# Copies out of PSUM kept back on ScalarE until the next step of another generator: a four-layer sparse graph kernel

## Chip, cores, metric

One core of one Trainium2 chip. The metric is device time in microseconds of one execution; lower is better.

## The reference, cut to what matters

```python
def _L0_gnn_ref(adj_matrix, h, Wq, Wk, Wv, Wo, bo, ...):       # also layers 2 and 3
    scores = einsum('bnhd,bmhd->bhnm', Q, K) / sqrt(HEAD_DIM)   # 8 heads of 16
    attn = softmax(where(adj == 0, -inf, scores))
    x = layer_norm(h + (attn @ V) @ Wo + bo)
    return layer_norm(x + relu(x @ W1 + b1) @ W2 + b2)
def _L1_gnn_ref(x, adj, W, a_src, a_dst, ...):                  # graph attention, then layer norm
```

x is (16, 1024, 128) in float32; a row of adj has about 8 neighbours in 1024. The kernel sorts the nodes by degree and gathers only the neighbours.

## The kernel before

Work goes in 64 units: 4 layers, 2 groups of graphs, 8 tiles of 128 nodes (t = 0 has the highest degrees, 7 the lowest; those with t from 3 to 6 are called quick). In a unit, VectorE forms products, sums and weighted products of gathered rows. The *tails* of the unit before run between them: output projection, norm, feed-forward, norm, projection for the next layer. A tail is a Python generator, one for each half (A and B) of the graphs, and B is one step behind A. The order in which they emit instructions is the order in which the traces show them on an engine (ScalarE has A's copy ahead of B's scalings, at 1688.05 and 1688.73 us).

```python
def normed(y):
    ...                                           # squares with sums, on ScalarE
    yield
    nc.gpsimd.tensor_tensor(rstd, total, power, ALU.pow)
    yield
    for i in range(GH):                           # "the four scalings", L422
        nc.scalar.activation(z[:, i, :], y[:, i, :], AF.Copy, scale=rstd[:, i : i + 1])
    return z

def turned(z, dst, gain=None, shift=None):
    ps = bank([P, GH, P])
    for i in range(GH):
        nc.tensor.transpose(ps[:, i, :], z[:, i, :], ident)
    if gain is None:
        nc.scalar.copy(dst, ps)                   # L431
    else:                                         # L433
        nc.scalar.activation(dst, ps, AF.Identity, bias=shift, scale=gain)
# ... (cut)
def attention_tail(l, g, t, h, o):
    for _ in range(h):                            # half B one step later
        yield
    # ... output projection, normed (cut)
    turned(z, x1, p["ln1_g"], p["ln1_b"])
    yield
    for f in range(F):                            # feed-forward: matmul L479, relu L483
        ...
    # ... second layer, normed (cut)
    yield from finish(...)                        # turned(z, xn, ...), then project(): kv, L371/L375
# ... (cut)
def exponentials(i):
    nc.vector.tensor_reduce(sc, ...)              # L614
    nc.scalar.activation(ex, sc, AF.Exp, ...)     # L618; weighted() on VectorE (L639) needs ex
# ... (cut)
def advance(gens):
    for gen in list(gens):
        if next(gen, "end") == "end":
            gens.remove(gen)
```

Of the kernel before, what the change touches and what calls it, by code (L numbers as in the profile page):

```python
# [15 lines left out]
AF = mybir.ActivationFunctionType  # L16
# [5 lines left out]
D = 128  # L22
# [23 lines left out]
GH = G // HF  # L46
# [30 lines left out]
def sparse_path(ctx: ExitStack, tc: tile.TileContext, a: dict, out: bass.AP, flag):  # L77


    nc = tc.nc  # L80
# [6 lines left out]
    def bank(shape):  # L87
        return banks.tile(shape, F32, tag="ps", name="ps")
# [270 lines left out]
    srcs = {}  # L359


    def project(l, g, t, h, x):

        nc.sync.dma_start(kept[l, g][t, :, h, :], x.rearrange("p g n -> p (g n)"))
        table = tables[l, g][t * P : (t + 1) * P, :]
        if LAYERS[l][1] is ATTN:
            kv = twos.tile([P, 2, GH, D], F32, tag="kv", name="kv")
            for i in range(0, GH, 2):
                ps = bank([P, 2, 2 * D])
                for k in range(2):  # L370
                    nc.tensor.matmul(  # L371
                        ps[:, k, :], x[:, i + k, :], w[LAYERS[l][0], "Wkv"],
                        start=True, stop=True,
                    )
                nc.scalar.copy(  # L375
                    kv[:, :, i : i + 2, :].rearrange("p c g d -> p g c d"),
                    ps.rearrange("p g (c d) -> p g c d", d=D),
                )
                yield
            nc.sync.dma_start(  # L380
                table.rearrange("p (c x) -> p c x", c=2)[:, :, h * GH * D : (h + 1) * GH * D],
                kv.rearrange("p c g d -> p c (g d)"),
            )
            return
        kv = twos.tile([P, GH * D + GH], F32, tag="kv", name="kv")
        if h == 0:
            srcs[g, t] = const.tile([P, G], F32, name=f"src{g}{t}")
        for i in range(0, GH, 2):
            ps = bank([P, 2, D + 2])
            for k in range(2):  # L390
                nc.tensor.matmul(ps[:, k, :], x[:, i + k, :], wg, start=True, stop=True)
            nc.scalar.copy(
                kv[:, i * D : (i + 2) * D].rearrange("p (g d) -> p g d", d=D), ps[:, :, :D]
            )
            to = GH * D + i
            nc.scalar.copy(
                kv[:, to : to + 2].rearrange("p (g o) -> p g o", o=1), ps[:, :, D : D + 1]
            )
            at = h * GH + i
            nc.scalar.copy(  # L400
                srcs[g, t][:, at : at + 2].rearrange("p (g o) -> p g o", o=1), ps[:, :, D + 1 :]
            )
            yield

        nc.sync.dma_start(table[:, h * GH * D : (h + 1) * GH * D], kv[:, : GH * D])
        nc.sync.dma_start(table[:, ROW + h * GH : ROW + (h + 1) * GH], kv[:, GH * D :])
# [18 lines left out]
    def turned(z, dst, gain=None, shift=None):  # L425

        ps = bank([P, GH, P])
        for i in range(GH):
            nc.tensor.transpose(ps[:, i, :], z[:, i, :], ident)  # L429
        if gain is None:  # L430
            nc.scalar.copy(dst, ps)  # L431
        else:
            nc.scalar.activation(dst, ps, AF.Identity, bias=shift, scale=gain)  # L433

    def over_graphs(v):
        return v.rearrange("p (o d) -> p o d", o=1).to_broadcast([P, GH, D])
# [17 lines left out]
    def attention_tail(l, g, t, h, o):  # L454
        layer = LAYERS[l][0]
        p = {n: w[layer, n] for n in ATTN if (layer, n) in w}
        xt = xs[l, g, t][:, h]
        for _ in range(h):
            yield
        oT = twos.tile([P, GH, P], F32, tag="oT", name="oT")  # L460
        turned(o, oT)
        yield
        ps = ybanks.tile([P, GH, D], F32, tag="yps", name="yps")
        for i in range(GH):
            nc.tensor.matmul(ps[:, i, :], oT[:, i, :], p["Wo"], start=True, stop=False)  # L465
            nc.tensor.matmul(ps[:, i, :], xt[:, i, :], centre, start=False, stop=True)
        yield
        y = twos.tile([P, GH, D], F32, tag="y", name="y")
        nc.vector.tensor_tensor(y, ps, over_graphs(p["bo"]), ALU.add)
        yield  # L470
        z = yield from normed(y)
        yield
        x1 = twos.tile([P, GH, P], F32, tag="oT", name="x1")
        turned(z, x1, p["ln1_g"], p["ln1_b"])
        yield
        f1 = ones_.tile([P, F, GH * P], F32, tag="f1", name="f1")
        for f in range(F):
            ps = bank([P, GH * P])
            nc.tensor.matmul(  # L479
                ps, p["W1"][:, f * P : (f + 1) * P], x1.rearrange("p g n -> p (g n)"),  # L480
                start=True, stop=True,
            )
            nc.scalar.activation(f1[:, f, :], ps, AF.Relu, bias=p["b1"][:, f : f + 1])  # L483
        yield
        ps = ybanks.tile([P, GH, D], F32, tag="yps", name="yps")
        for i in range(GH):
            for f in range(F):
                nc.tensor.matmul(  # L488
                    ps[:, i, :], f1[:, f, i * P : (i + 1) * P], p["W2"][:, f, :],
                    start=(f == 0), stop=False,  # L490
                )
            nc.tensor.matmul(ps[:, i, :], x1[:, i, :], centre, start=False, stop=True)  # L492
        yield
        z = yield from normed(ps)
        yield
        yield from finish(l, g, t, h, z, p["ln2_g"], p["ln2_b"])
# [40 lines left out]
    def is_attention(u):  # L537
        return LAYERS[units[u][0]][1] is ATTN
# [12 lines left out]
    def queries(u):  # L551

        l, g, t = units[u]
        if not is_attention(u):
            ps = bank([P, J, G])
            for j in range(J):
                nc.tensor.matmul(ps[:, j, :], rep_of(j, True), srcs[g, t], start=True, stop=True)
            ofs[u] = smalls.tile([P, J, G], F32, tag="of", name="of")
            nc.scalar.copy(ofs[u], ps)
            return  # L560
        qs[u] = reps.tile([P, J, ROW], F32, tag="qr", name="qr")
        for h in range(HF):
            q = ones_.tile([P, GH * D], F32, tag="q", name="q")
            ps = bank([P, GH, D])
            for i in range(GH):
                nc.tensor.matmul(
                    ps[:, i, :], xs[l, g, t][:, h, i, :], w[LAYERS[l][0], "Wq"],
                    start=True, stop=True,
                )
            nc.scalar.copy(q, ps.rearrange("p g d -> p (g d)"))  # L570
            yield
            pss = []
            for j in range(J):
                ps = bank([P, GH * D])
                nc.tensor.matmul(ps, rep_of(j), q[32 * j : 32 * j + 32], start=True, stop=True)  # L575
                pss.append(ps)
            for j in range(J):
                nc.scalar.copy(qs[u][:, j, h * GH * D : (h + 1) * GH * D], pss[j])  # L578
            yield

    def gathered(i):
# [22 lines left out]
    def exponentials(i):  # L604
# [8 lines left out]
        if is_attention(u):  # L613
            nc.vector.tensor_reduce(  # L614
                sc[:, :n, :], prs[i][0][:, :n, :].rearrange("p k (a d) -> p k a d", d=HD),
                mybir.AxisListType.X, ALU.add,
            )
            nc.scalar.activation(ex, sc[:, :n, :], AF.Exp, scale=1.0 / HD**0.5)  # L618
        else:
            nc.vector.tensor_tensor(  # L620
                sc[:, :n, :], es[i][:, :n, ROW:], ofs[u][:, j : j + n, :], ALU.add
            )
            nc.vector.scalar_tensor_tensor(
                sc[:, :n, :], sc[:, :n, :], SLOPE, sc[:, :n, :], ALU.mult, ALU.max
            )
            nc.scalar.activation(ex, sc[:, :n, :], AF.Exp)
# [45 lines left out]
    def divided(u):  # L672

        l, g, t = units[u]
        heads, d = (H, HD) if is_attention(u) else (1, D)
        den = bank([P, G * heads])
        for r, n in enumerate(ROUNDS[t]):
            for j in range(n):
# [25 lines left out]
    slow = []  # L704

    def advance(gens):
        for gen in list(gens):
            if next(gen, "end") == "end":
                gens.remove(gen)

    pace = [0.0, 0.0]

    def others():
        pace[0] += pace[1]
        while pace[0] >= 1.0:
            advance(tails)
            pace[0] -= 1.0
        if fronts:
            advance(fronts)
        elif slow:  # L720
            advance(slow)

    with tc.manual_schedule():
        for _ in first(0):
            pass
        loaded(0)
        loaded(1)
        for _ in queries(0):
            pass
        slow.append(first(1))  # L730
        for i in range(AHEAD):
            gathered(i)
# [2 lines left out]
        for i in range(len(parts) + 1):  # L735
# [43 lines left out]
            if ends:  # L779

                while fronts:
                    advance(fronts)
        while tails:
            advance(tails)
        for _ in closing:
# [437 lines left out]
```

## Time and profile before

| | us |
|---|---|
| time, median of 4 | 3033.95 (3027.94 to 3037.83) |
| VectorE busy, TensorE busy | 2150, 2125 |
| ScalarE busy, GpSimd busy | 1424, 1478 |
| VectorE's idle before L639, waiting for `ex` of L618 | 333 |

A wait line reads: engine and line that waited, who ended the wait, us in total, number of waits, the longest. A timeline line reads: start, length, engine, line, operation, out<-in, shape, and in square brackets the idle just before and its releaser. The lines themselves stand in the prediction.

### The profile page before, as it was taken

The page shows a single profiled execution, that of the slowest core. Times are in us where ns is not written, and L with a number is a line of the kernel's source. Part 1 is how long each engine was busy: PE and PEld are TensorE (multiplying, and loading weights), DVE is VectorE, ACT ScalarE, POOL GpSimd, SP SyncE. Part 2 cuts the span into 40 slices and gives each one's busy share as a digit, 9 for nine tenths or more (in the row PEclk, how much of TensorE's full clock was granted, in tenths as well). Part 3 has the DMA queues.
Part 4 walks back from the last instruction along what each step waited for, and adds up shares of the span by engine and source line. Part 5 has one row for each costly group of instructions (what it writes and reads, how often), then busy time and mean ns, then how long its engine had stood idle before and what let it go on. Part 6 is the DMA issues. An engine that isn't in the chain of part 4 may idle for free.

```text
span 3034.5 us, 35305 instructions
## 1 busy us (share of the span) xinstructions
PE 2124.9 (70%) x12569; PEld 1325.2 (44%) x12569; DVE 2150.0 (71%) x1493; ACT 1424.2 (47%) x4468; POOL 1478.1 (49%) x1086
## 2 busy tenths in 40 slices
PE   1365767776777786766577887777877676766766
PEld 1343444543554443434245554555544444334444
DVE  7505768768887666675798767887678877778772
ACT  1033445563556544435345664456543555334454
POOL 0123435443444568685335443354435577466673
PEclk9986888887888888988788988889887888787887
DMA  1057766545555468777665654656546553355540
GB/s 56 12 181 287 304 215 236 204 169 217 223 225 179 171 210 288 256 272 282 221 238 216 228 205 179 271 218 230 200 183 245 198 216 145 144 219 210 195 144 22
DMA packets 171144, 615.36 MB, mean 203 GB/s; under 512 B 44472, under 2 KB 47928, under 8 KB 122462
## 3 DMA queue, kind: packets, MB, share of 16 engines
q0 software_dynamic: 99584, 480.93, 43.4%
q1 hardware_dynamic: 71376, 132.10, 11.9%
q8 instruction: 101, 1.65, 0.2%
q14 instruction: 83, 0.68, 0.1%
HBM read 650.67 MB, written 100.73 MB: 248 GB/s over the span
## 4 chain that ended last, share of the span: by engine, by line
PE 40%; DVE 15%; ACT 14%; POOL 11%; issue 10%; DMA 8%; another core or an unknown queue 0%; SPq 0%; POOLq 0%; DVEq 0%; ACTq 0%
PE ps L479 7%; PE yps L488 6%; PE ps L429 5%; ACT z L413 5%; POOL e L591 5%; PE acc L666 5%; POOL rstd L419 4%; DVE sc L614 4%; DMA xg<-in_x,places 3%; DVE pr L639 3%; PE ps L371 3%; DVE pr L600 3%; ACT qr L578 3%; PE yps L465 3%; PE yps L492 3%
## 5 line engine op out<-in xcount | busy, mean ns | idle before, releaser
L591 POOL DMA_INDIRECT e<-table,idx x656 | 886.1, 1351 | 448.1 <-DVE pr L639 263.4
L639 DVE TENSOR_TENSOR pr<-e,ex 128x2048 f32<-128x2048 f32 (+1 forms) x344 | 760.1, 2216 | 338.7 <-ACT ex L618 333.4
L419 POOL TENSOR_TENSOR rstd<-total,power 128x4 f32<-128x4 f32 x224 | 359.9, 1608 | 753.4 <-ACT z L413 718.9
L600 DVE TENSOR_TENSOR pr<-e,qr 128x2048 f32<-128x2048 f32 (+1 forms) x258 | 565.1, 2190 | 195.1 <-ACT qr L578 138.1
L666 PE MATMUL acc<-pr,marks 128*32 128x512 f32 x2624 | 467.7, 701 | 146.5 <-DVE pr L639 136.6
L614 DVE TENSOR_REDUCE sc<-pr 128x128 f32<-128x2048 f32 (+1 forms) x258 | 561.9, 2178 | 0.0
L429 PE MATMUL ps<-ident,z 128*128 128x128 f32 x768 | 199.4, 368 | 246.5 <-ACT z L422 246.5
L429 PEld LDWEIGHTS ps<-ident,z 128*128 128x128 f32 x768 | 126.5, 172 | 396.2 <-ACT z L422 325.7
L371 PE MATMUL ps<-Wkv,xT 128*128 128x256 f32 x768 | 244.5, 466 | 41.5 <-ACT xT L431 21.2
L479 PE MATMUL ps<-x,W 128*128 128x512 f32 x384 | 241.1, 761 | 41.8 <-ACT x L433 41.8
L488 PE MATMUL yps<-W,f 128*128 128x128 f32 x1536 | 258.5, 287 | 13.0 <-ACT f L483 11.0
L666 PEld LDWEIGHTS acc<-pr,marks 128*32 128x32 f32 x2624 | 89.4, 120 | 398.5 <-issue 213.8
L488 PEld LDWEIGHTS yps<-W,f 128*128 128x128 f32 x1536 | 212.5, 197 | 69.9 <-ACT f L483 44.3
L483 ACT ACTIVATE f<-ps,b 128x512 f32<-128x512 f32 x192 | 131.4, 687 | 230.8 <-PE ps L479 230.0
L578 ACT COPY qr<-ps 128x512 f32<-128x512 f32 x384 | 197.6, 596 | 74.9 <-PE ps L575 74.7
L413 ACT ACTIVATE z<-y,root 128x128 f32<-128x128 f32 x512 | 198.5, 396 | 50.6 <-DVE y L506 35.4
L575 PE MATMUL ps<-q,rep 32*128 32x512 f32 x768 | 169.7, 679 | 67.4 <-ACT oT L431 41.3
L371 PEld LDWEIGHTS ps<-Wkv,xT 128*128 128x128 f32 x768 | 166.2, 231 | 91.2 <-ACT xT L431 29.3
L618 ACT ACTIVATE ex<-sc 128x128 f32<-128x128 f32 (+1 forms) x258 | 81.1, 314 | 253.6 <-DVE sc L614 236.1
L465 PE MATMUL yps<-Wo,oT 128*128 128x128 f32 x768 | 180.2, 322 | 7.5 <-ACT oT L431 6.9
L375 ACT COPY kv<-ps 128x512 f32<-128x512 f32 x192 | 112.5, 587 | 140.9 <-PE ps L371 129.4
L413 ACT ACTIVATE z<-yps,root 128x128 f32<-128x128 f32 x384 | 135.6, 368 | 77.2 <-PE yps L492 77.2
(128 smaller groups left out, 2977.8 us busy)
## 6 DMA issues: line engine op xcount, KB each, us to landing
table<-kv SPq DMA_DIRECT2D x96, 512.0 KB
kept<-xT SPq DMA_DIRECT2D x128, 256.0 KB
x<-kept SPq DMA_DIRECT2D x64, 512.0 KB
e<-table,idx POOLq DMA_INDIRECT x656
table<-kv SPq DMA_DIRECT2D x32, 256.0 KB
edges<-in_adj SPq DMA_DIRECT2D x8, 512.0 KB
W<-in_L_gnn_W SPq DMA_DIRECT2D x6, 128.0 KB
xg<-in_x,places POOLq DMA_INDIRECT x32
```

Source lines behind the costliest of these rows:

```text
L371: nc.tensor.matmul(ps[:, k, :], x[:, i + k, :], w[LAYERS[l][0], "Wkv"], start=True, stop=True,)
L413: nc.scalar.activation(z[:, i, :], y[:, i, :], AF.Square, scale=D**-0.5, bias=root, accum_out=total[:, i : i + 1],)
L419: nc.gpsimd.tensor_tensor(rstd, total, power, ALU.pow)
L429: nc.tensor.transpose(ps[:, i, :], z[:, i, :], ident)
L479: nc.tensor.matmul(ps, p["W1"][:, f * P : (f + 1) * P], x1.rearrange("p g n -> p (g n)"), start=True, stop=True,)
L488: nc.tensor.matmul(ps[:, i, :], f1[:, f, i * P : (i + 1) * P], p["W2"][:, f, :], start=(f == 0), stop=False,)
L578: nc.scalar.copy(qs[u][:, j, h * GH * D : (h + 1) * GH * D], pss[j])
L591: nc.gpsimd.indirect_dma_start(out=es[i][:, k, :], out_offset=None, in_=tables[l, g][:, :], in_offset=bass.IndirectOffsetOnAxis(ap=idx[:, ...
L600: nc.vector.tensor_tensor(prs[i][0][:, :n, :], es[i][:, :n, :ROW], qs[u][:, j : j + n, :], ALU.mult)
L614: nc.vector.tensor_reduce(sc[:, :n, :], prs[i][0][:, :n, :].rearrange("p k (a d) -> p k a d", d=HD), mybir.AxisListType.X, ALU.add,)
L639: nc.vector.tensor_tensor(prs[i][k0 // 2][:, :m, :].rearrange("p k (a d) -> p k a d", d=d), es[i][:, k0 : k0 + m, base : base + ROW].rearr ...
L666: nc.tensor.matmul(accums[u][32 * j : 32 * j + 32, h, :], marks[:, CHUNK[t, r, j], :], tiles[j // 2][:, j % 2, h * GH * D : (h + 1) * GH * D],
```

## The change

The intent: a copy out of PSUM (the `ps` that TensorE's matmuls write) has to wait for TensorE (50.0 us of ScalarE's idle before L433 in the kernel before), and ScalarE, which works in order in the trace (the `ex` at 1708.31 us began only after two copies, with its sums done since 1702.93), waits with it. So the copy is kept back and given to ScalarE later, at the next opening of a step (`advance`) or just ahead of the next attention exponential, so that other ScalarE work can go first.

```diff
+    pending = []
+    def flush():
+        while pending:
+            pending.pop(0)()
+    def later(fn, *args, **named):
+        pending.append(lambda: fn(*args, **named))
...
-            nc.scalar.activation(dst, ps, AF.Identity, bias=shift, scale=gain)
+            later(nc.scalar.activation, dst, ps, AF.Identity, bias=shift, scale=gain)
... (likewise the copies of kv, oT, f1, q, qr, of)
+            flush()
             nc.scalar.activation(ex, sc[:, :n, :], AF.Exp, scale=1.0 / HD**0.5)
...
     def advance(gens):
+        flush()
         for gen in list(gens):
... (flush also in others, divided, queries; others steps its front directly)
```

## The prediction

> **What bounds the kernel now.** I read the page first (parts 1, 2, 4, 5), then who waited for whom, then the timelines of ScalarE, TensorE, GpSimd and VectorE in one stretch that repeats.

> ```profile
> PE 2124.9 (70%) x12569; PEld 1325.2 (44%) x12569; DVE 2150.0 (71%) x1493; ACT 1424.2 (47%) x4468; POOL 1478.1 (49%) x1086
> PE 40%; DVE 15%; ACT 14%; POOL 11%; issue 10%; DMA 8%; another core or an unknown queue 0%; SPq 0%; POOLq 0%; DVEq 0%; ACTq 0%
> ```

> No engine is full, and the chain that ended last passes from engine to engine: the kernel is bound by waits between engines. The longest waits say which:

> ```profile
> DVE pr L639 <- ACT ex L618: 333.4, 128, 8.9
> PE ps L429 <- ACT z L422: 246.5, 94, 9.4
> ACT ex L618 <- DVE sc L614: 236.1, 59, 18.6
> ACT z L422 <- POOL rstd L419: 80.4, 49, 5.0
> PE ps L479 <- ACT x L433: 41.8, 46, 2.7
> ```

> VectorE waits 333.4 us for exponentials, in 128 of 258 places; the exponential itself waits for VectorE's sums only 59 times. So mostly an exponential is late because ScalarE works in order and has the layer tail's work in front of it. What delays a ScalarE instruction in front of such an exponential delays VectorE by as much. (The whole of L600's waits for `qr`, 138.1 us, has one of 103.1 us in it, the start.)

> [...] the `ex` at 1708.31 us began only after two copies, with its sums done since 1702.93. [...] The clock record agrees: it is only ever 1 or 0.5, and section 2 shows 0.7 to 0.9 as means. [...] the power (L419) took 1.04 us where it began ahead of a product of VectorE (1698.36 against 1698.44), 3.04 us where it began under one (L600, two inputs, 1702.85 to 1705.13). This makes some `rstd` late, which matters below.

> **The change part by part.** It adds and removes no work. I compared the order of the two programs on each engine, line numbers and buffer numbers left out. TensorE, VectorE, GpSimd and the DMA queue have the same instructions in the same order. On ScalarE, 132 of 4,123 instructions change places with something, in two ways.

> (a) 96 times (48 attention tails with `x1`, 32 with `xT` to the next layer, 16 graph tails) the copy of half A's transposes, with gain and shift (L433, 0.78 us), now stands after the four scalings of half B (L422, 1.27 us together) and no longer before them. Everywhere else a copy kept back meets only other copies kept back before the next opening, so the order stays.

> (b) 27 copies or so, nearly all in graph units, now stand after an exponential of graph attention instead of before it. VectorE waited for those exponentials only 5.0 us altogether (L639 on L626, 46 of them), so (b) is worth at most some 3 us.

> For (a), the first kind. ScalarE, then TensorE, then VectorE:

> ```profile
> 1686.35 1.28 ACT L422 ACTIVATE z<-y,rstd 128x128 f32<-128x128 f32 x4
> 1688.05 0.78 ACT L433 ACTIVATE x<-ps,ln_b,ln_g 128x512 f32<-128x512 f32 x1 [0.42 <-PE ps L429]
> 1688.73 1.27 ACT L422 ACTIVATE z<-y,rstd 128x128 f32<-128x128 f32 x4
> ...
> 1698.08 0.33 ACT L618 ACTIVATE ex<-sc 128x128 f32<-128x128 f32 x1
> ```

> ```profile
> 1688.88 1.99 PE L479 MATMUL ps<-x,W 128*128 128x512 f32 x4 [0.87 <-ACT x L433]
> 1690.70 0.60 PE L429 MATMUL ps<-ident,z 128*128 128x128 f32 x4
> ```

> ```profile
> 1698.44 2.29 DVE L639 TENSOR_TENSOR pr<-e,ex 128x2048 f32<-128x2048 f32 x1 [5.26 <-ACT ex L618]
> ```

> The idle that the change fills is the 0.42 us before the copy. But TensorE's next work, the feed-forward matmul at 1688.88, waits for this copy, and B's transposes stand behind that matmul in TensorE's own order: the row at 1690.70 has no wait for `z`. So finishing B's scaling earlier frees nobody, and the copy goes from 1688.05 to 1687.63 + 1.17 = 1688.80 us: 0.75 us later. From there everything is a chain (matmul, `f`, second layer, half B, squares, `ex`), and VectorE was already waiting 5.26 us at its end. So +0.75 us, whole.

> The second kind, where `rstd` of B is late (rows of ScalarE, GpSimd, TensorE):

> ```profile
> 1702.59 0.78 ACT L433 ACTIVATE xT<-ps,ln_b,ln_g 128x512 f32<-128x512 f32 x1 [0.42 <-PE ps L429]
> 1706.07 1.14 ACT L422 ACTIVATE z<-yps,rstd 128x128 f32<-128x128 f32 x4 [2.70 <-POOL rstd L419]
> 1707.09 0.60 ACT L375 COPY kv<-ps 128x512 f32<-128x512 f32 x1
> 1707.63 0.78 ACT L433 ACTIVATE xT<-ps,ln_b,ln_g 128x512 f32<-128x512 f32 x1
> 1708.31 0.30 ACT L618 ACTIVATE ex<-sc 128x128 f32<-128x128 f32 x1
> ```

> ```profile
> 1702.99 3.04 POOL L419 TENSOR_TENSOR rstd<-total,power 128x4 f32<-128x4 f32 x1
> ```

> ```profile
> 1703.42 1.13 PE L371 MATMUL ps<-Wkv,xT 128*128 128x256 f32 x4 [0.87 <-ACT xT L433]
> 1706.49 1.10 PE L429 MATMUL ps<-ident,z 128*128 128x128 f32 x4 [1.94 <-ACT z L422]
> ```

> Now the copy at 1702.59 was done in the shadow of the power. After the change it stands behind scalings that wait for the power: it starts at 1707.11, 4.5 us later. Then one after the other: copy to 1707.9, projection (L371, 1.13) to 1709.1, B's transposes (0.6 to 0.75) to 1709.7, B's copy (its next can start after 0.68), `ex` at 1710.4 instead of 1708.31. So +2.1 us, and VectorE was waiting there (3.51 us).

> I did this same shift for each of the 96 places from their own rows: new start of the copy, the projection's own length, 0.75 us for the transposes, less what time VectorE had left after that exponential before its L639.
> - 48 `x1`: 38 of them have VectorE waiting at the next exponential; 0.74 to 0.79 us in the quicker units, 0.91 to 1.17 in the others. Sum 33.1 us.
> - 32 `xT` of attention: 12 of the late kind at 1.6 to 3.0 us (24 us together), four with 1.7 us where VectorE waited only 0.16 us, the rest 0 to 1. Sum 37.7 us.
> - 16 graph tails: mostly 4 to 15 us of slack before the next use; sum 4.1 us.

> Together 75 us, an upper figure, as a later wait may give some back: I take nine tenths, 67 us. Less 3 us of (b). In the late kind TensorE now stands idle some 5 us between A's transposes and the projection, instead of 0.87 us, so its clock should halve there: projection and transposes twice as long, about 0.5 us in 12 places, 6 us. Sum: +70 us, 3035.6 + 70 = 3105.6; I say 3105.

> **The rivals.** *The intended gain*: ScalarE no longer stands before its queue's head waiting for TensorE. For it: the idle before L433 is 56 us, before L431 (L429's copies) 243 us. Against it: only the 0.42 us and the like before 96 copies of L433 is filled, 41 us in sum, and L431, L483 and L578 keep their place, as nothing given directly comes between them and the next opening. Even if all 41 us were gained, 2995; with losses half as large as I say, about 3035. *Slack swallows it*: VectorE is 71% busy, and gathers or the power may have been about to bound a unit anyway; the waits for gathered rows are only 56.1 us at L600 and 42.0 at L620, so I doubt it. Half of it swallowed: 3070. *PSUM*: copies given later hold the four banks longer. TensorE's order and the buffers' rotation are the same, and only copies of L433 are late; so nothing beyond the sum. *Runaway*: idle TensorE at half clock, in more places than 12, lengthens L479 and L488 in the chain; each 1% on TensorE's 40% of the chain is 12 us: 3130.

> **Range and chances.** All in all 3105, and 3065 to 3135 for 8 in 10: below, half of the loss hidden; above, the clock. The limit for slower by over 2% is 3096, close below my number: slower 0.61, within 2% 0.36, faster 0.03.

> **What would show it.** Right: all busy times but TensorE's within 1%; VectorE's wait at L639 for L618 up by about 60 us from 333; ScalarE's idle before L433 on TensorE down from 50.0 to near 10; L479's wait for `x` (41.8) up by 30 or more, and L371/L391's for `xT` (18.5 and 17.1) several times as long; in units like the one at 1702 us the copy of A directly behind B's scalings. Step by step wrong: if L639's wait stays at 333, the copies were not on the path; if L422's wait for `rstd` fell, the power isn't what makes B late; if the waits for gathered rows shrink by as much as L639's grow, slack swallowed it. A time under 3035 would mean that B's earlier scaling does free something that I hold to be behind the matmul.

## The result

3114.99 us, median of 4 (3110.0 to 3129.27), against 3033.95. The ratio is 1.0277, 95% interval 1.0236 to 1.0317: slower. A ratio here is the mean time of one kernel's fast runs over that of the other's in the same rounds, so not quite the ratio of the medians. The profiled run took 3108.2 us, 73.7 more than the profiled run of before.

In the changed kernel the copies all carry L369, the line of the helper, and other lines have moved: L433 and L483 are now L369, L422 is L435, L479 is L492, L371 is L380, L618 is L633, L639 is L654. The changed kernel's busy times first:

```profile
PE 2132.1 (69%) x12569; PEld 1332.7 (43%) x12569; DVE 2148.0 (69%) x1493; ACT 1420.3 (46%) x4468; POOL 1473.0 (47%) x1086
```

The busy times are the same to 0.4%, TensorE's 7 us longer. What grew is waiting; here is who waited for whom in the changed kernel:

```profile
DVE pr L654 <- ACT ex L633: 424.4, 125, 9.2
...
ACT ex L633 <- DVE sc L628: 238.6, 66, 18.8
...
PE ps L442 <- ACT z L435: 214.2, 80, 11.1
...
ACT z L435 <- POOL rstd L432: 123.8, 71, 8.2
...
PE ps L380 <- ACT xT L369: 85.6, 51, 5.4
...
PE ps L492 <- ACT x L369: 72.7, 47, 2.4
```

VectorE waits 91 us longer for exponentials (333.4 to 424.4), although the exponentials wait no longer for VectorE (236.1 to 238.6). The feed-forward matmul waits 31 us longer for `x` (41.8 to 72.7). The intended saving is there, and it is small: ScalarE's idle before L433 on the transposes fell from 50.0 to 15.6 us.

One quick unit of the changed kernel, the counterpart of those in the prediction (layer L2, tile 5). ScalarE's timeline around `x1`:

```profile
1801.88 2.45 ACT L435 ACTIVATE z<-y,rstd 128x128 f32<-128x128 f32 x8
1804.21 0.78 ACT L369 ACTIVATE x<-ps,ln_b,ln_g 128x512 f32<-128x512 f32 x1
1806.58 0.69 ACT L369 ACTIVATE f<-ps,b 128x512 f32<-128x512 f32 x1 [1.59 <-PE ps L492]
```

and around `xT`:

```profile
1818.47 1.16 ACT L435 ACTIVATE z<-yps,rstd 128x128 f32<-128x128 f32 x4
1823.53 1.14 ACT L435 ACTIVATE z<-yps,rstd 128x128 f32<-128x128 f32 x4 [3.90 <-POOL rstd L432]
1824.54 0.80 ACT L369 ACTIVATE xT<-ps,ln_b,ln_g 128x512 f32<-128x512 f32 x1
1827.51 0.59 ACT L369 COPY kv<-ps 128x512 f32<-128x512 f32 x1 [2.17 <-PE ps L380]
1828.36 0.78 ACT L369 ACTIVATE xT<-ps,ln_b,ln_g 128x512 f32<-128x512 f32 x1 [0.27 <-PE ps L442]
1829.04 0.30 ACT L633 ACTIVATE ex<-sc 128x128 f32<-128x128 f32 x1
```

Both halves are scaled in one run (x8), and only then is A's copy made. In the second stretch A's copy, which was made in the shadow of the power, stands behind scalings that wait 3.90 us for it. The same unit on TensorE and on VectorE:

```profile
1805.04 3.21 PE L492 MATMUL ps<-x,W 128*128 128x512 f32 x4 [1.50 <-ACT x L369]
...
1825.39 2.08 PE L380 MATMUL ps<-Wkv,xT 128*128 128x256 f32 x4 [5.23 <-ACT xT L369]
```

```profile
1815.90 2.29 DVE L654 TENSOR_TENSOR pr<-e,ex 128x2048 f32<-128x2048 f32 x1 [7.19 <-ACT ex L633]
...
1829.37 2.29 DVE L654 TENSOR_TENSOR pr<-e,ex 128x2048 f32<-128x2048 f32 x1 [6.78 <-ACT ex L633]
```

VectorE's two waits are 7.19 and 6.78 us where they were about 5.26 and 3.51. There is a second thing to see: the same four matmuls of L492 take 3.21 us instead of 1.98 or so, and those of L380 2.08 instead of 1.13. TensorE itself is slower here: over these two rows the granted clock is 0.60 and 0.50, over the rows of L479 and L371 in the prediction 1.00.

To see where the time went I took each unit's length from VectorE's timeline (from its division `o<-acc` to the next unit's, the stretch in which its tails run), added up by kind of unit and compared with the kernel before. "Predicted" is the sum of the places in that group as worked out for the prediction, ahead of its last corrections (the total: 75 us).

| units | before, us | predicted | changed | e1 | e3 (x1) | e4 (xT) |
|---|---|---|---|---|---|---|
| L0, t 0-2 (6) | 319.9 | +8.3 | +11.5 | +1.2 | +5.4 | +8.0 |
| L0, t 3-6 (8) | 327.6 | +17.2 | +19.2 | +0.2 | -0.7 | +16.6 |
| L2, t 0-2 (6) | 289.2 | +13.8 | +17.6 | +0.6 | +7.9 | +14.4 |
| L2, t 3-6 (8) | 327.3 | +20.4 | +31.5 | -0.5 | +21.7 | +21.5 |
| L3, t 0-2 (6) | 306.8 | +5.8 | +1.3 | -0.9 | -0.2 | -0.8 |
| L3, t 3-6 (8) | 326.6 | +5.4 | +10.2 | -0.1 | +11.5 | 0.0 |
| L1, graph (16) | 425.3 | +4.1 | -8.6 | -3.6 | +3.4 | +3.5 |

(e1, e3 and e4 are experiments below. The units with t = 7 and the lead-in are left out; they scatter by up to 10 us. Together with the end they are 9 us shorter in the changed kernel and 8 in e1, so the column "changed" sums to 83 us where the profiled runs differ by 74.)

### The profile page after: what moved, and what is told of

It is laid out like the page before. It is cut to its first block, busy times and chain, and to the rows that moved or that the text cites. A ratio compares the mean times of both kernels' runs of the same rounds, so it can differ in the third digit from the quotient of the medians.

```text
span 3108.2 us, 35279 instructions
## 1 busy us (share of the span) xinstructions
PE 2132.1 (69%) x12569; PEld 1332.7 (43%) x12569; DVE 2148.0 (69%) x1493; ACT 1420.3 (46%) x4468; POOL 1473.0 (47%) x1086
## 4 chain that ended last, share of the span: by engine, by line
PE 36%; ACT 17%; DVE 12%; POOL 11%; issue 9%; DMA 6%; POOLq 0%; DVEq 0%; SPq 0%; ACTq 0%
PE ps L492 7%; ACT z L426 6%; PE yps L501 6%; PE acc L681 5%; POOL rstd L432 5%; ACT z L435 5%; POOL e L605 5%; DVE sc L628 4%; DVE pr L654 3%; PE ps L380 3%; DVE pr L614 3%; DMA e<-table,idx 3%; PE ps L442 3%; ACT qr L369 3%; PE yps L505 3%
## 5 line engine op out<-in xcount | busy, mean ns | idle before, releaser
L654 DVE TENSOR_TENSOR pr<-e,ex 128x2048 f32<-128x2048 f32 (+1 forms) x344 | 760.7, 2218 | 429.3 <-ACT ex L633 424.4
L614 DVE TENSOR_TENSOR pr<-e,qr 128x2048 f32<-128x2048 f32 (+1 forms) x258 | 565.6, 2192 | 196.5 <-ACT qr L369 144.3
L681 PE MATMUL acc<-pr,marks 128*32 128x512 f32 x2624 | 460.9, 692 | 136.1 <-DVE pr L654 126.0
L380 PE MATMUL ps<-Wkv,xT 128*128 128x256 f32 x768 | 250.6, 475 | 86.2 <-ACT xT L369 85.6
L492 PE MATMUL ps<-x,W 128*128 128x512 f32 x384 | 249.8, 786 | 72.7 <-ACT x L369 72.7
L369 ACT ACTIVATE f<-ps,b 128x512 f32<-128x512 f32 x192 | 131.4, 687 | 285.1 <-PE ps L492 285.0
L501 PEld LDWEIGHTS yps<-W,f 128*128 128x128 f32 x1536 | 213.0, 197 | 68.5 <-ACT f L369 42.1
L369 ACT COPY kv<-ps 128x512 f32<-128x512 f32 (+2 forms) x320 | 140.2, 460 | 208.4 <-PE ps L380 162.2
L369 ACT COPY qr<-ps 128x512 f32<-128x512 f32 x384 | 197.5, 596 | 75.3 <-PE ps L589 72.6
L380 PEld LDWEIGHTS ps<-Wkv,xT 128*128 128x128 f32 x768 | 168.8, 235 | 137.3 <-ACT xT L369 106.3
L633 ACT ACTIVATE ex<-sc 128x128 f32<-128x128 f32 (+1 forms) x258 | 81.1, 314 | 249.4 <-DVE sc L628 238.6
L435 ACT ACTIVATE z<-y,rstd 128x128 f32<-128x128 f32 x512 | 160.4, 394 | 32.4 <-POOL rstd L432 32.3
```

The source lines that it names most:

```text
L369: pending.append(lambda: fn(*args, **named))
L380: nc.tensor.matmul(ps[:, k, :], x[:, i + k, :], w[LAYERS[l][0], "Wkv"], start=True, stop=True,)
L492: nc.tensor.matmul(ps, p["W1"][:, f * P : (f + 1) * P], x1.rearrange("p g n -> p (g n)"), start=True, stop=True,)
L501: nc.tensor.matmul(ps[:, i, :], f1[:, f, i * P : (i + 1) * P], p["W2"][:, f, :], start=(f == 0), stop=False,)
L614: nc.vector.tensor_tensor(prs[i][0][:, :n, :], es[i][:, :n, :ROW], qs[u][:, j : j + n, :], ALU.mult)
L654: nc.vector.tensor_tensor(prs[i][k0 // 2][:, :m, :].rearrange("p k (a d) -> p k a d", d=d), es[i][:, k0 : k0 + m, base : base + ROW].rearr ...
```

## The experiments

Theory: the loss is the 96 places in which B's scalings now stand ahead of A's copy. Rivals: the other effects of keeping copies back (part (b), PSUM banks, new waits); slack; and TensorE's clock. Every kernel was run beside the kernel before on one chip; the twelve fell into three groups, in which the kernel before had medians of 3028.9 (e1, e3, e4, e7), 3035.0 (e5, e6, e9, e10) and 3028.1 us (e8, e11, e12, e13).

### e1: copies ahead of the scalings again, all else as changed

```diff
+        flush()
         for i in range(GH):
             nc.scalar.activation(z[:, i, :], y[:, i, :], AF.Copy, scale=rstd[:, i : i + 1])
```

> The changed kernel with one line more: all copies kept back are given before half B's four scalings. This puts back the 96 places of part (a) exactly and keeps part (b), everything else as changed. My theory (the loss is the 96 places): within 10 us of the kernel before, 3025 to 3045, VectorE's wait for the attention exponential back to about 333 us (before) from 424 (changed). Rival (part (b), PSUM banks held longer, or semaphores of the new order cost something by themselves): it stays near 3115, or stops in between.

Measured: 3030.4 us, ratio 1.0004 (0.9978 to 1.003). The wait in the first fence of the result is back:

```profile
DVE pr L655 <- ACT ex L634: 330.0, 124, 8.9
```

One line undoes the whole loss. The rest of the change (27 or so copies behind graph exponentials, the openings, the longer hold on the banks) is worth nothing that can be measured (0.3% would have shown).

### e3 and e4: the two kinds of place alone

```diff
-            nc.scalar.activation(dst, ps, AF.Identity, bias=shift, scale=gain)
+            give(nc.scalar.activation, dst, ps, AF.Identity, bias=shift, scale=gain)
 # e3: give=later for x1 alone; e4: give=later for xn alone; every other copy given at once
```

> Of all copies only the 48 pairs of x1 are kept back, the rest is given at once as in the kernel before. Theory: 33 us of loss, all of the small kind (0.75 to 1.17 us each), ratio 1.011, about 3067. Rival (only the places with a late power cost anything, and small shifts are swallowed by slack): ratio 1.000. Rival (feed-forward is where it all happens): the whole 80 us, ratio 1.027.

Measured: 3080.1 us, ratio 1.0163 (1.0136 to 1.019): 49 us, not 33.

> Of all copies only those of xT (to the next layer, 32 pairs of attention and 16 of graph tails) are kept back. Theory: 42 us from the places and some 6 us from TensorE's half clock, ratio 1.015 (3080), and the wait of the scalings for the power up from 80 to about 124 us, as in the changed kernel. With e3 the two should sum to the changed kernel's 80 us if the places are independent. Rival (slack swallows xT): ratio 1.000 to 1.005.

Measured: 3085.18 us, ratio 1.0179 (1.0151 to 1.0206): 54 us, somewhat over the 48. The scalings' wait for the power is 120.5 us, near the 124 expected.

Neither rival holds: both kinds cost, and neither is swallowed as a whole. But e3 costs half as much again as its places, and the two do not add up (1.63 and 1.79% against 2.77%). The table shows where: e3's eight quick units of L2 lost 21.7 us, and the same eight units of L0, with the same instructions up to the next projection, lost nothing. The busy view by stretch shows what is different there. Columns are stretch, its length, busy us (instructions) of TensorE, its weight loads, VectorE, ScalarE, GpSimd, then TensorE's granted clock (1.00 is full speed), DMA share and GB/s. The unit L2, tile 5, before:

```profile
1754.20:1794.30 40.10, 32.38 (x209) 20.88 (x208) 29.78 (x17) 25.71 (x77) 18.80 (x14) 0.96 0.50 173
```

and in e3:

```profile
1768.30:1812.70 44.40, 37.12 (x210) 23.68 (x209) 29.82 (x18) 25.69 (x77) 18.82 (x14) 0.81 0.47 162
```

The clock fell from 0.96 to 0.81. In the corresponding unit of L0 it is 0.92 in both kernels, and that unit grew by 0.4 us. e3's feed-forward matmul of A in this unit:

```profile
1786.30 3.78 PE L495 MATMUL ps<-x,W 128*128 128x512 f32 x4 [1.50 <-ACT x L369]
```

It takes 3.78 us where it took 1.98. The idle before it grew only from 0.87 to 1.50 us, in the wake of another of 0.97 us that was there before as well.

```profile
1766.34:1769.76 3.42, 2.45 (x19) 0.68 (x11) 3.26 (x2) 3.42 (x11) 2.93 (x2) 1.00 0.08 33
1769.76:1773.17 3.41, 2.54 (x9) 1.25 (x9) 3.41 (x3) 2.77 (x8) 3.10 (x2) 1.00 0.24 38
```

and in e3, where the first is 55% busy (1.88 of 3.41 us) and the next at half clock:

```profile
1781.95:1785.36 3.41, 1.88 (x12) 0.55 (x4) 3.25 (x2) 3.41 (x12) 3.23 (x2) 1.00 0.00 0
1785.36:1788.77 3.41, 2.47 (x3) 1.18 (x4) 3.41 (x3) 1.24 (x3) 2.15 (x2) 0.50 0.47 108
```

So a gap of 1.50 us is no limit by itself. A's feed-forward matmuls ran at full clock (1.98 us) in 4, 5 and 2 of the eight quick units of L0, L2 and L3 before, in 6, 0 and 0 in e3, and in 1, 0 and 2 in the changed kernel. e3's quick units of L0 have the same gap, and their stretches came to 56% and more; why that sufficed there and 55 to 56% did not in L2 stays open.

### e9 and e11: the idle filled

If the clock is the cause, filling that idle must bring the time back although ScalarE's order stays bad. The x1 transposes are done three times, into the same bank; the second and third time lie in the shadow of B's scalings.

```diff
-        for i in range(GH):
-            nc.tensor.transpose(ps[:, i, :], z[:, i, :], ident)
+        for _ in range(times):            # e9: 3 for every x1
+            for i in range(GH):           # e11: 3 for half A and t >= 3, else 1
+                nc.tensor.transpose(ps[:, i, :], z[:, i, :], ident)
```

> e3 (only x1 kept back) cost 49 us where the places sum to 33, and its quick units of the third layer grew by 2.5 to 4.3 us each where 0.75 was due: there the granted clock fell from 0.88 to 0.96 to 0.81 and half A's feed-forward matmuls took 3.8 in place of 2.0 us; in the same units of the first layer the clock stayed at 0.92 and they grew by only 0.4 us. Theory (clock): TensorE's idle between A's transposes and that matmul, 0.87 before and 1.50 us now, takes the clock to half. Here the x1 transposes are done three times over in the shadow of B's scalings, which only fills that idle: the quick units of the third layer should come back to 41 to 42 us and the ratio fall from 1.016 to 1.009 to 1.012. Rival (the order itself costs more than I worked out): 1.016 or more.

Measured: 3109.51 us, ratio 1.024 (1.0217 to 1.0262). The total is a miss. L2's tiles 3 to 5 came out as expected: they are back at 41 to 42.5 us (the two that I looked at have a clock of 0.88 and 0.92; tile 6 is not back, 45.1 and 44.4), and so is the matmul:

```profile
1808.30 1.98 PE L496 MATMUL ps<-x,W 128*128 128x512 f32 x4 [0.87 <-ACT x L369]
```

What I had not thought of: half B has nobody's shadow, so its fill lies in TensorE's path (B's transposes take 1.47 us or more, against 0.60 to 1.06 in e3); and most units with t from 0 to 2 are at half clock at this place with or without the fill (17 of 18 in e3, 14 in e9), so there the fill costs time and gains nothing (L3, t = 1: 51.8 to 54.4 us). Hence e11.

> e9 mended. In e9 the quick units came back (44.4 to 42.1 us, half A's feed-forward matmuls 3.78 to 1.98 us), but the fill for half B lies in TensorE's path (0.6 to 1.5 us), and the first three units of each group, cold before and after (clock 0.75 to 0.77), grew by 3 us each. Here e3's x1 transposes are done three times for half A alone and in units 3 to 7 alone. Theory (clock): e3's extra loss in the quick units goes, ratio 1.008 to 1.012 against e3's 1.016. Rival (order alone): 1.016 or more.

Measured: 3049.87 us, ratio 1.007 (1.005 to 1.009) against e3's 1.0163. So the clock was about half of what keeping back x1 cost. Perhaps somewhat less: the fill leaves TensorE warmer than the kernel before (A's feed-forward at full clock in 22 of the 24 quick units, against 11), and e12 below shows that warming TensorE in these units also gains 0.3% on the order of the kernel before. What is left, 21 us, is below the sum of the places (33 us), perhaps for this reason and as L3's first units had swallowed theirs.

### e5 and e6: no scaling waits for the power (wrong results on purpose)

```diff
-            nc.scalar.activation(z[:, i, :], y[:, i, :], AF.Copy, scale=rstd[:, i : i + 1])
+            nc.scalar.activation(z[:, i, :], y[:, i, :], AF.Copy, scale=power[:, i : i + 1])
 # e5: in the kernel before; e6: in the changed kernel; power is a constant column
```

> Wrong result on purpose: the kernel before, with the scalings of both halves taking a constant column in place of rstd, so that no scaling waits for GpSimd's power (which still runs). Same order on every engine. It is the base for e6. Theory: the scalings' waits for rstd, 80 us, go away; most of them stood in front of an exponential, so 40 to 70 us faster than the kernel before (2960 to 2990).

> Wrong result on purpose: the changed kernel with the same constant column. Theory: the loss against e5 is only the scalings' own 0.7 to 1.2 us in the 96 places (x1 33 us as before; 48 xT at 0.6 to 0.9, mostly exposed) and TensorE's clock; in place of 80 us it should be about 50 to 60 (ratio e6 to e5 1.016 to 1.020). Rival 1 (the late power is most of the loss): under 30 us. Rival 2 (the power has no part): 80 us again.

Measured: e5 2986.51 us, ratio 0.9849 (0.9824 to 0.9874); e6 3047.34 us, ratio 1.0049 (1.0025 to 1.0074). e6 over e5 is 1.0049 / 0.9849 = 1.020, or 61 us between the medians, where the change costs 81 with the power. So about 20 us of the loss are the late power and three quarters do not need it; both differences are known to some 11 us each, so the 20 are rough. That fits the places: the 12 late ones were to cost about 2.0 us each where a plain swap costs 0.75, and 12 times the difference is 15 us.

### e7 and e8: the exponential ahead of copies

The waits suggest a use of the same tool: give copies *behind* the exponential. Both are e1 with this.

```diff
# e7: the exponential ahead of everything kept back
-            flush()
             nc.scalar.activation(ex, sc[:, :n, :], AF.Exp, scale=1.0 / HD**0.5)
# e8: only kv copies have a list of their own, which stays behind
+            flush(ahead=True)             # all but the kv copies
             nc.scalar.activation(ex, sc[:, :n, :], AF.Exp, scale=1.0 / HD**0.5)
```

> Copies before scalings (as e1), and the attention exponential is given before the copies kept back, not after them. If VectorE's 333 us of waiting come from work standing in front of the exponential in ScalarE's order, taking the f, kv, q and qr copies from in front of it (some 400 pairs) should gain: 30 to 60 us against the kernel before, 2975 to 3005, with the wait at L639 well below 300 us. Rival (the exponential then holds up the copies where VectorE's sums are late, and TensorE and the queries behind them): no gain, or slower by up to 1%, with ScalarE's wait for the sums far over 236 us.

Measured: 3054.73 us, ratio 1.008 (1.0056 to 1.0103): the rival. In e7 the waits changed places:

```profile
ACT ex L633 <- DVE sc L629: 367.8, 105, 17.8
...
DVE pr L654 <- ACT ex L633: 267.3, 79, 8.1
```

VectorE does wait 66 us less for exponentials, but ScalarE stands 132 us longer before them, waiting for sums, with copies behind it that TensorE needs: its wait for `q` rose from 25.9 to 78.0 us.

> e1 with the kv copies alone (they go to a table that is read a layer later) given behind the attention exponential, 60 pairs; every other copy stays ahead of it, unlike e7. Theory (ScalarE's order in front of the exponential): 5 to 25 us faster than the kernel before, ratio 0.992 to 0.998. Rival (the copies free PSUM banks that TensorE needs, as e7 may have shown): 1.000 to 1.008.

Measured: 3020.87 us, ratio 0.9974 (0.9954 to 0.9995): a small gain, as expected. kv is the one copy that nobody waits for within the unit.

### e10, e12 and e13: TensorE kept warm

```diff
+        if warm:                          # e10: every scaled half; e12, e13: t >= 3
+            for i in range(2 * GH):
+                nc.tensor.transpose(ps[:, i % GH, :], ident, ident)
         for i in range(GH):
             nc.tensor.transpose(ps[:, i, :], z[:, i, :], ident)
```

> e1 (order of the kernel before) with eight transposes of the identity ahead of the transposes of every scaled half, into the same bank, overwritten after; they need no data and fall where TensorE waits for the scalings (246 us in 94 waits). If TensorE's clock is part of the bound, the granted clock rises from about 0.84 to 0.88 or more and the kernel gains 15 to 45 us (ratio 0.985 to 0.995). Rival: the eight take 0.9 to 1.8 us of TensorE where it is not idle, or the clock does not move: ratio 1.000 to 1.015.

Measured: 3060.99 us, ratio 1.0095 (1.0069 to 1.012): the rival's time. But the clock did move: the other five runs of e10 have 0.861 to 0.869. The profiled one has 0.845, as before (0.846), only because its first 100 us, with the same little work for TensorE, were at 0.66 in place of 1.00; from 300 to 2850 us it has 0.87 against 0.84. So it is the first half of the rival that held, the transposes in TensorE's path. L2's tiles 3 to 5 came to 39.9 us, at a clock of 0.96 and 1.00 in two of them, but those with t from 0 to 2 went from 47.8 to about 51.3 us.

> e10 with the eight idle transposes in units 3 to 7 alone, where e10's units were 39.9 and 40.9 us against 39.8 to 42.3 and 40.4 to 42.5 of the kernel before, and not in units 0 to 2, where they took 51.3 against 47.8. Theory (clock): 8 to 20 us faster than the kernel before, ratio 0.993 to 0.998. Rival (e10's good units came from the shift of their surroundings): 1.000 or more.

Measured: 3018.97 us, ratio 0.9969 (0.995 to 0.9989), clock 0.869: as expected.

> e8 and e12 together, as a candidate that beats both kernels. If both gain on their own, the sum: 15 to 40 us faster than the kernel before, ratio 0.987 to 0.995. If e8 loses, then in between.

Measured: 3012.59 us, ratio 0.9946 (0.9925 to 0.9968). e13, with the copies in the order of the kernel before, kv behind the exponential and TensorE kept warm in the quick units, is the fastest kernel of this study that is correct, 0.5% below the kernel before.

## Why the prediction was right

- **The order comparison** (96 places, nothing else moved that matters): right, and e1 shows it: 1.0004 with the 96 places put back. The traces show the same 48, 32 and 16 copies moved (of 4,468 ScalarE instructions by the profile's count, not 4,123).
- **B's earlier scaling frees nobody, as B's transposes stand behind A's matmul**: right; A's next matmul waits 31 us longer and of the groups in the table only the graph units grew shorter (by 8.6 us, 3.6 in e1 too).
- **The size, +70 us**: the measured difference is 81 of medians and 74 of profiled runs. The sum is nearly right for partly wrong terms, so how near it came is in part luck. "Slack gives a tenth back" stood for L3's first units, which swallowed 4.5 of 5.8 us, and the graph units, 12.7 under their term (3.6 of these are in e1 as well).
- **The clock, 6 us in 12 places**: the mis-sized term. I put it in the late-power places alone, with their 5 us of idle; that a shorter gap would do no harm was my estimate and not shown, and in e3 a stretch of 3.41 us that was 55% busy was followed by half clock (see e3; the means in section 2 reach down to 0.6, not 0.7). Even for the late places the sum was too small: projection and transposes twice as long is some 1.7 us (1.13 and 0.6), not 0.5, or 20 us in 12 places. They do show it (L380: 1.13 to 2.08 us, at a clock of 1.00 and 0.50). And it also struck at `x1`, where the idle grew from 0.87 to 1.50 us: e3 lost 1.63% and, with that idle filled in the quick units, 0.7%. I had this as the "runaway" rival, at 1% of TensorE's chain; it came true in the quick units of L2 and L3, which lost 41.7 us where 25.8 were due.
- **The late power**: right in kind and, roughly, in size; 20 us by e5 and e6. The scalings' wait for `rstd` rose from 80.4 to 123.8 us. I had only said that it must not fall.
- **VectorE's wait at L639 up by about 60 us**: 91, more than the time itself grew by.
- **Slack**: the sign named against it held; the waits for gathered rows hardly shrank (56.1 to 52.1 and 42.0 to 41.8 us).
- **The intended gain**: 34 us of ScalarE's idle before L433 did go, and none of it was on the path.
- *Open*: why e3 and e4 lose more apart than together. The ratios add up to 0.65% more than the whole, just outside their intervals. In the quick units of L2 the parts lost 21.7 and 21.5 us and the whole 31.5; perhaps both pay for a colder TensorE, and it cannot be made cold twice at the same place, but that is not shown: I have no run that separates this.

## What to carry to other kernels

Before work is put ahead of an instruction that waits, ask who waits for that instruction and whether anyone waits for what goes ahead. Here a wait of 0.42 us was filled with 1.2 us of work that was useless until later, in front of a copy on which TensorE, then ScalarE, then VectorE hung. Hold back what has no reader nearby (kv), not what heads a chain. And compare the orders of the two programs engine by engine: a diff of forty lines came down to one swap in 96 places, which can be priced from the timeline of the kernel before.
